# A ternary convolution's activations in SBUF: six pairs of quarter buffers for five, and one padded image for each channel half

## The chip, the cores and the metric

The kernel runs on one core of a Trainium2 chip. TensorE is called PE here, VectorE DVE, ScalarE ACT, GpSimd POOL and SyncE SP. PEld is PE's weight load. The metric is the device time of one execution in microseconds (us), of which lower is better. `L1357` is line 1357 of the kernel before.

## What is computed

Four layers follow each other on x of shape [4, 256, 64, 64] (images, channels, rows, columns), all in float32. Each is a residual layer behind a group normalisation:

```python
# --- layer 0: axial attention, 1: ternary conv, 2: binary grouped conv, 3: expanded conv
x = x + _L0_conv_ref(_gn(x), ...)
x = x + _L1_conv_ref(_gn(x), weight, alpha, bias)
x = x + _L2_conv_ref(_gn(x), ...)
x = x + _L3_conv_ref(_gn(x), ...)
```

The change lies in layer 1. Its weights take the values 1, 0 and -1 (times alpha):

```python
def _L1_conv_ref(x, weight, alpha, bias):
    delta = 0.7 * mean(abs(weight))
    ternary = where(w > delta, 1.0, where(w < -delta, -1.0, 0.0))
    w_t = ternary * alpha
    out = conv_general_dilated(x, w_t, (1, 1), padding=[(1, 1), (1, 1)])   # 3x3, NCHW
    return out + bias[None, :, None, None]

def _gn(v, G=32, eps=1e-5):     # over 8 channels and all rows and columns of one image
    return (g - mean(g)) / sqrt(var(g) + eps)
```

A group norm needs the sums of a whole image before the first row of that image can be normalised.

## The kernel before

The program runs the layers one after the other, each in a phase with buffer pools of its own. A pool takes its place in SBUF when it is opened, and a pool of a later phase may lie over the memory of an earlier one, whose last use it then waits for. The framework keeps the order of reads and writes on each buffer and arranges the instructions of each engine by its own scheduling, starting from the order in which the program emits them. So the lines below give the order of emission. The order on an engine can differ from it.

Layer 1 works on **quarters**: 16 rows of one image, 1024 pixels, in two channel halves t of 128 partitions. Four images of four quarters make 16 quarters, or 32 half quarters. The names are these:

- `load(b, t, q)` (L1264) makes x after layer 0 for one half quarter. It fetches the input into `dx` (L145, from `in_x`), fetches two attention results into `a` (two DMAs of L1276 for one, L145 for the other), scales one on ACT (L1279) and adds both to dx on DVE (L1281, L1284; the second also sums the pixels). `square` (L1262) sums the squares on ACT. All four DMAs of a load go through SP's queue.
- `row_of` (L1256) chooses the slot for dx: `2 * ((q - b) % 5) + t`, ten slots, which are five pairs. The slot of quarter (b+1, q) is therefore the one that quarter (b, q-1) had.
- `norm(b, ts)` (L1289) joins the sums of an image (L1298, and L1105 to L1110 in a helper), averages over groups with small matmuls on PE (`pst`, L115, L125 and L126) and forms scale and bias (L1303 to L1306).
- `transform(b, t, q)` (L1309) writes the normalised rows into a padded image `d_pad` on ACT (L1322: 16 rows, and one row from each neighbouring quarter), forms four combinations `dv` of 8x66 from them on DVE (L1324, L1328, L1329; a minimal-filtering scheme over rows), and splits these into `dh` (fp32r copy on ACT, L1334) and `dl` (what is left, on DVE, L1335).
- `chunk(b, q, co)` (L1340) makes one output half of one quarter: 48 matmuls 128x128 by 128x512 (L1357; four combinations, two input halves, dh and dl, three columns), the inverse combination (L1372 on ACT, L1373, L1374, L1376 on DVE), and the residual sum into dx (L1381). Then dx is written to `x2_d` for layer 2 (L1386), and for co = 1 to `z_d` as well (L1388). Both are DMAs of POOL's queue.

There are four padded images before: two with 18 rows for inner quarters (0 and 1, one for each half), and two with 19 rows for the first and last quarters of an image (2 and 3), in which the top or bottom row stays zero.

The loop (L1407 to L1418) emits, for each quarter (b, q), the loads of both halves of (b+1, q), the norm of the next image ahead of the last quarter, and then for each half the transform of the next quarter and the chunk of this one. The four loads of the first image stand ahead of the loop. A slot can be refilled only when L1386 and L1388 have read it.

Layer 2's phase (`e_` pools, from L1471) comes next. It reads x2_d and z_d back, and its first matmuls (L1451) take the operand `e_tr` (L1440).

Of the kernel before, what the change touches and what calls it, by code (L numbers as in the profile page):

```python
# [9 lines left out]
F32 = mybir.dt.float32  # L10
# [8 lines left out]
P = 128  # L19
B = 4  # L20
C = 256
HW = 4096
# [19 lines left out]
def network(ctx: ExitStack, tc, x, wqkv, relm, relt, relw, relv, counts, masks, vecs, rowv, ab, w1, l2w1, l2w2, l3w, mats, out):  # L42
# [4 lines left out]
    nc = tc.nc  # L47
# [94 lines left out]
    def load_shuffled(dst, src, t):  # L142

        rows = src.rearrange("(two i) f -> i two f", two=2)[64 * t : 64 * t + 64]
        nc.sync.dma_start(out=dst, in_=rows)  # L145
# [20 lines left out]
    with ExitStack() as ph:  # L166
# [112 lines left out]
        for b in range(B):  # L279
            xs, gm, rs = ready  # L280
            qs = [qp.tile([P, 8, 8, 64], F32, name=f"qs{t}_{b}", tag="qs") for t in range(2)]
            for k in range(NB):
# [49 lines left out]
                if k in (3, 7) and 2 * b + k // 4 - 1 in range(len(pieces)):  # L332
                    i = 2 * b + k // 4 - 1
# [76 lines left out]
    with ExitStack() as ph:  # L410
# [224 lines left out]
        for b in range(B):  # L635
            for gp in range(GP):
# [3 lines left out]
                q = qs[j]  # L640
                o = op.tile([P, 32, 64, 2], F32, name=f"o_{b}_{gp}", tag="o")
# [65 lines left out]
        s2, _ = bn_affine(sp, mean, var, row[:, 0:48], row[:, 48:96], 48)  # L707
# [36 lines left out]
    def from_scores(general, keep):  # L744
# [482 lines left out]
        with ExitStack() as ph:  # L1227
            ps_ = {
                k: pool(ph, f"d_{k}", {"a": 3, "o": 2}.get(k, 1))
                for k in "x2 x3 a x4 x5 x0 x6 p2 v0 h00 l00 u0 u1 x1 o s v1 h10 l10 h11 l11 p0 p1 p3 x7 x8 x9 h01 l01".split()  # L1230
            }
            ap_, op, sp = ps_["a"], ps_["o"], ps_["s"]
            wide = pool(ph, "d_ps3", 1, PSUM)
# [1 line left out]
            ring = [pool(ph, "d_ps", 2, PSUM)] * 2 + [wide]  # L1235
            taken = [0]

            pads = [
                ps_[f"p{i}"].tile([P, 18 + i // 2, 66], F32, name=f"d_pad{i}", tag="pad") for i in range(4)
            ]  # L1240
            u = [ps_[f"u{t}"].tile([P, 3, 4, C], F32R, name=f"d_u{t}", tag="u") for t in range(2)]
            for t in range(2):
                nc.vector.memset(pads[t][:, :, 0], 0.0)
                nc.vector.memset(pads[t][:, :, 65], 0.0)
                edge = pads[2 + t]
                nc.vector.memset(edge[:, 0:19:18, :], 0.0)
                nc.vector.memset(edge[:, 1:18, 0], 0.0)
                nc.vector.memset(edge[:, 1:18, 65], 0.0)

            def load_weights(t):  # L1250
                for dx in range(3):
# [2 lines left out]
            xs, vs, sums, mvs, norms, shift = {}, {}, {}, {}, {}, {}  # L1254

            def row_of(b, t, q):  # L1256
                xs[b, t, q] = ps_[f"x{2 * ((q - b) % 5) + t}"].tile([P, HW // 4], F32, name=f"dx_{b}_{t}_{q}", tag="x")
                return xs[b, t, q]

            def square(src, out):  # L1260
# [3 lines left out]
            def load(b, t, q):  # L1264

                if (b, t) not in sums:
                    sums[b, t] = sp.tile([P, 4, 2], F32, name=f"dst_{b}_{t}", tag=f"st{t}", bufs=2)
                xt = row_of(b, t, q)
                load_shuffled(xt, x[b][:, bass.ts(q, HW // 4)], t)
                if b == 0 and t == 1 and q == 0:  # L1270
                    for two in range(2):
                        prs[t, two] = value_norm(t, two, pst, "pst")
                a = ap_.tile([P, HW // 4], F32, name=f"a1_{b}_{t}_{q}", tag="a")
                for two in range(2):
                    src = at_d[1][b][t * P + 64 * two : t * P + 64 * two + 64].rearrange("i (k f) -> i k f", k=4)
                    nc.sync.dma_start(  # L1276
                        out=a[two:P:2].rearrange("p (k f) -> p k f", k=4), in_=src[:, :, bass.ts(q, 256)]
                    )
                nc.scalar.activation(a, a, AF.Copy, scale=prs[t, 1][:, 0:1])  # L1279
                xv = xt.rearrange("p (n k i) -> p n k i", k=4, i=16)  # L1280
                nc.vector.tensor_tensor(xv, a.rearrange("p (k n i) -> p n k i", k=4, i=16), xv, ALU.add)  # L1281
                a = ap_.tile([P, HW // 4], F32, name=f"a0_{b}_{t}_{q}", tag="a")
                load_shuffled(a, at_d[0][b][bass.ts(t, P), bass.ts(q, HW // 4)], 0)
                nc.vector.scalar_tensor_tensor(  # L1284
                    xt, a, prs[t, 0][:, 0:1], xt, ALU.mult, ALU.add, accum_out=sums[b, t][:, q, 0:1]
                )
                square(xt, sums[b, t][:, q, 1:2])

            def norm(b, ts):  # L1289

                if b not in mvs:
                    mvs[b] = small(sp, [P, 2, 2])
                for t in range(ts.start, ts.stop):
                    if b == 0:
                        shift[t] = small(keep, [P, 1])
                        nc.vector.tensor_tensor(shift[t], prs[t, 0][:, 1:2], prs[t, 1][:, 1:2], ALU.add)
                    whole_stats(sp, mvs[b][:, t, :], sums[b, t])
                    nc.vector.tensor_tensor(mvs[b][:, t, 0:1], mvs[b][:, t, 0:1], shift[t], ALU.add)  # L1298
                gm, rs = norm_stats(sp, pst, mvs[b], ts, M_GRPS, "d")
                for t in range(ts.start, ts.stop):  # L1300
                    i = t - ts.start
                    ra = small(sp, [P, 1])
                    nc.vector.tensor_tensor(ra, rs[:, i : i + 1], row[:, 96:97], ALU.mult)  # L1303
                    nb = small(sp, [P, 1])
                    nc.vector.tensor_tensor(nb, shift[t], gm[:, i : i + 1], ALU.subtract)
                    nc.vector.tensor_tensor(nb, nb, ra, ALU.mult)  # L1306
                    norms[b, t] = nb, ra

            def transform(b, t, q):  # L1309


                nb, ra = norms[b, t]
                edge = q in (0, 3)
                pad = pads[2 + t if edge else t]
                pad = pad[:, 1:19] if q == 3 else pad[:, 0:18]
                parts = [(xs[b, t, q].rearrange("p (h w) -> p h w", w=64), slice(1, 17))]
                if q > 0:
                    parts.append((xs[b, t, q - 1][:, 15 * 64 :].rearrange("p (h w) -> p h w", w=64), slice(0, 1)))
                if q < 3:
                    parts.append((xs[b, t, q + 1][:, 0:64].rearrange("p (h w) -> p h w", w=64), slice(17, 18)))  # L1320
                for src, rows in parts:
                    nc.scalar.activation(pad[:, rows, 1:65], src, AF.Identity, bias=nb, scale=ra)  # L1322
                v = ps_[f"v{t}"].tile([P, 4, 8, 66], F32, name=f"dv_{b}_{t}_{q}", tag="v")
                nc.vector.tensor_tensor(  # L1324
                    v[:, 0:4:3].rearrange("p k q w -> p q k w"), pad[:, 0:16].rearrange("p (q k) w -> p q k w", k=2),
                    pad[:, 2:18].rearrange("p (q k) w -> p q k w", k=2), ALU.subtract,
                )
                nc.vector.tensor_tensor(v[:, 1], pad[:, 1:17:2], pad[:, 2:18:2], ALU.add)  # L1328
                nc.vector.tensor_tensor(v[:, 2], pad[:, 2:18:2], pad[:, 1:17:2], ALU.subtract)  # L1329
                hi, lo = (  # L1330
                    ps_[f"{k}{(4 * b + q) % 2}{t}"].tile([P, 4, 8, 66], F32R, name=f"d{k}_{b}_{t}_{q}", tag="tr")
                    for k in "hl"
                )
                nc.scalar.copy(hi, v)  # L1334
                nc.vector.tensor_tensor(lo, v, hi, ALU.subtract)  # L1335
                vs[b, t, q] = hi, lo
# [67 lines left out]
            load_weights(1)  # L1404
            norm(0, slice(1, 2))
            transform(0, 1, 0)
            for b in range(B):  # L1407
                for q in range(4):
                    if b + 1 < B:
                        for t in range(2):  # L1410
                            load(b + 1, t, q)
                        if q == 3:
                            norm(b + 1, slice(0, 2))
                    nxt = (b, q + 1) if q < 3 else (b + 1, 0)
                    for co in range(2):
                        if nxt[0] < B:
                            transform(nxt[0], co, nxt[1])
                        chunk(b, q, co, b == q == co == 0)  # L1418
            lost = None
            if not general:  # L1420
                far = small(keep, [P, 1])
# [49 lines left out]
        with ExitStack() as ph:  # L1471
# [17 lines left out]
            pads = [[(padp if t == h == 1 else padq).tile([P, 34, 66], BF16, name=f"e_pad{t}{h}", tag=f"pad{t}{h}")  # L1489
                     for h in range(2)] for t in range(2)]  # L1490
# [6 lines left out]
            for i, p_ in enumerate((wp1, wp2)):  # L1497
                k = p_.tile([P, 2, 3, 4, 3, 64], BF16, name=f"e_k{i}", tag="k")
# [213 lines left out]
            _, sy2, cy2 = sums_affine(1, vec[:, V_G3 : V_G3 + 1], vec[:, V_B3 : V_B3 + 1])  # L1712


        with ExitStack() as ph:
# [37 lines left out]
            def finish_3(b, h, co, xh, sp, pst):  # L1753
                nc.gpsimd.dma_start(out=out[b, bass.ts(co, P), bass.ts(h, HW // 2)], in_=xh)

            set_up, load_weights, prepare, norm, transform, rest, sp, pst = conv_layer(
                "g", ph, u3_d, "a x0 x1 x2 x3 x4 x5 o u0 u1 t2 t3 t4 s t0 p0 p1 t1 t5", M_GRP, load_3,
                vec[:, V_L3B : V_L3B + 2], (1, 0), finish_3,
            )
# [131 lines left out]
```

## Time and profile before

| what | value |
|---|---|
| median of 3 runs | 2771.07 us |
| range of these runs | 2767.38 to 2775.86 us |
| the profiled execution | 2766.54 us |
| its span (first to last instruction) | 2764.8 us |
| mean granted TensorE clock | 0.937 |
| PE, share of the span busy | 87% |
| DVE, share of the span busy | 72% |
| ACT, share of the span busy | 44% |
| first and last matmul of L1357 | 1485.0 and 1908.9 us |

The profile is that of one execution, and its times count from its first instruction. The granted clock is the share of full speed that PE was allowed, and "busy" leaves out instructions that only issue DMAs or wait. Layer 1's convolution takes about 425 us of the span. The shares above are averages over all four layers and say little of this one stage.

### The profile page before, as it was taken

How to read it: one execution, taken by the hardware profiler on the slowest of the kernel's cores; microseconds unless marked ns; L12 is line 12 of the kernel's file. 1: busy time of each engine (PE TensorE's matmuls, PEld its weight loads, DVE VectorE, ACT ScalarE, POOL GpSimd, SP SyncE). 2: the span in 40 equal slices, each digit the busy share in tenths (PEclk: the TensorE clock that was granted, in tenths of full speed). 3: DMA queues.
4: the chain of work that ended last, by engine and by line, in shares of the span. 5: the costliest groups of instructions: out<-in, count | busy, mean ns of one | idle time of the engine just before them, and what ended most of it. 6: DMA issues, size and time to landing. Idle time of an engine off the chain costs nothing.

```text
span 2764.8 us, 78125 instructions
## 1 busy us (share of the span) xinstructions
PE 2398.3 (87%) x34632; PEld 1576.4 (57%) x34632; DVE 1980.3 (72%) x3362; ACT 1205.8 (44%) x1984; POOL 105.4 (4%) x201
## 2 busy tenths in 40 slices
PE   7999788888997888888773998998979859999998
PEld 4566555556665666666662776776545424444443
DVE  6665788988775466666558788885888877967742
ACT  4555355555555544555435466553448421110100
POOL 0000100000001000000000000000000000000000
PEclk9999899999999888899886999999989979999999
DMA  6766366666667777778776546524337742324110
GB/s 239 258 201 205 89 190 163 172 168 186 155 150 159 244 251 249 256 242 274 232 234 220 186 154 201 189 101 158 126 128 265 288 159 91 138 105 137 46 42 36
DMA packets 287996, 489.87 MB, mean 177 GB/s; under 512 B 32736, under 2 KB 149088, under 8 KB 274848
## 3 DMA queue, kind: packets, MB, share of 16 engines
q1 hardware_dynamic: 224992, 359.52, 42.9%
q10 hardware_dynamic: 48256, 58.73, 6.2%
q0 software_dynamic: 14400, 66.53, 6.1%
q8 instruction: 273, 4.47, 0.7%
q14 instruction: 75, 0.61, 0.1%
HBM read 281.46 MB, written 203.23 MB: 175 GB/s over the span
## 4 chain that ended last, share of the span: by engine, by line
issue 38%; PE 30%; DVE 14%; DMA 11%; ACT 5%; POOL 1%; SPq 1%; DVEq 0%; ACTq 0%; POOLq 0%
PE pd L505 5%; PE dc L1357 4%; PE po L293 3%; PE pv L308 3%; PE pq L526 3%; DMA at_d<-o_False 2%; PE e_False L867 2%; DMA x<-x_d 2%; PE pr_False L936 2%; DVE pt L877 2%; PE pe_False L970 2%; DMA dx<-in_x 2%; PE den_False L918 2%; PE pa_False L945 2%; PE pc L1451 2%
## 5 line engine op out<-in xcount | busy, mean ns | idle before, releaser
L1066 PE MATMUL gc<-gtr,g_u 128*128 128x512 f32 x1152 | 503.4, 599 | 11.3 <-DVE gtr L1044 6.7
L1066 PEld LDWEIGHTS gc<-gtr,g_u 128*128 128x128 f32 x1152 | 219.3, 191 | 287.3 <-issue 269.4
L512 DVE STREAM_TRANSPOSE t<-pd 128x1024 f32<-128x1024 f32 x256 | 304.5, 1229 | 86.0 <-PE pd L505 80.7
L505 PE MATMUL pd<-rm,qb 64*32 64x256 f32 x8192 | 305.5, 389 | 41.4 <-DVE t L512 32.3
L1451 PE MATMUL pc<-e_tr,e_k 128*64 128x512 bf16 x2304 | 265.3, 391 | 20.5 <-DVE e_tr L1440 13.3
L532 ACT ACTIVATE o<-pq 128x512 f32<-128x512 f32 x256 | 150.6, 594 | 267.0 <-PE pq L526 264.8
L1357 PE MATMUL dc<-dh,d_u 128*128 128x512 f32 x768 | 233.5, 414 | 33.9 <-ACT dh L1334 33.8
L505 PEld LDWEIGHTS pd<-rm,qb 64*32 64x32 f32 x8192 | 168.4, 108 | 134.7 <-DVE t L512 57.4
L907 ACT ACTIVATE pt<-pt,sm 128x512 f32<-128x512 f32 x256 | 162.7, 710 | 174.9 <-DVE pt L877 174.8
L1357 PE MATMUL dc<-dl,d_u 128*128 128x512 f32 x768 | 229.3, 408 | 0.4 <-DVE dl L1335 0.2
L1451 PEld LDWEIGHTS <-e_k 128*64 128x64 bf16 x2304 | 145.5, 112 | 137.2 <-issue 28.9
L526 PEld LDWEIGHTS pq<-t,t 64*64 64x64 f32 x8192 | 146.0, 138 | 86.1 <-issue 71.6
L526 PE MATMUL pq<-t,t 64*64 64x64 f32 x8192 | 168.5, 225 | 28.6 <-issue 23.5
L1357 PEld LDWEIGHTS dc<-dh,d_u 128*128 128x128 f32 x768 | 148.6, 195 | 74.9 <-ACT dh L1334 35.8
L877 DVE TENSOR_TENSOR pt<-e_False,si_False 128x1024 f32<-128x1024 f32 x128 | 151.6, 1216 | 34.6 <-PE e_False L867 34.3
L1357 PEld LDWEIGHTS dc<-dl,d_u 128*128 128x128 f32 x768 | 145.7, 191 | 42.2 <-DVE dl L1335 4.1
L1084 ACT COPY gc_c<-gc 128x512 f32<-128x512 f32 x32 | 18.6, 582 | 344.0 <-PE gc L1066 344.0
L867 PE MATMUL e_False<-qc_False,rw 32*128 32x256 f32 x1024 | 131.1, 481 | 27.4 <-DVE pt L877 15.8
L538 ACT ACTIVATE sq<-o 128x1024 bf16<-128x1024 f32 x128 | 135.5, 1059 | 4.0
L293 PE MATMUL po<-xg,wt 128*128 128x512 f32 x256 | 120.8, 611 | 6.1 <-DVE st L300 4.5
L970 PE MATMUL pe_False<-pt,ve 128*32 128x64 f32 x4096 | 91.4, 244 | 39.9 <-issue 31.8
L308 PE MATMUL pv<-wt,xg 128*128 128x256 f32 x512 | 120.0, 382 | 0.0
(403 smaller groups left out, 3604.5 us busy)
## 6 DMA issues: line engine op xcount, KB each, us to landing
si_False<-qk_d SPq DMA_DIRECT2D x64, 1024.0 KB
qk_d<-o SPq DMA_DIRECT2D x496, 128.0 KB
x<-x_d SPq DMA_DIRECT2D x32, 1056.0 KB
xa<-in_x SPq DMA_DIRECT2D x16, 1024.0 KB
vt_d<-vs ACTq DMA_DIRECT2D x32, 512.0 KB
q_d<-qs SPq DMA_DIRECT2D x64, 256.0 KB
qb<-q_d SPq DMA_DIRECT2D x128, 128.0 KB
qc_False<-q_d SPq DMA_DIRECT2D x64, 256.0 KB
```

The lines of the kernel that those rows point to most:

```text
L293: nc.tensor.matmul(psf, lhsT=wt[:, t, bass.ts(o, P)], rhs=xg[:, t, :], start=(t == 0), stop=(t == 1))
L308: nc.tensor.matmul(pv[:, j, :], lhsT=xg[:, t, pix], rhs=wt[:, t, C : 2 * C], start=(t == 0), stop=(t == 1),)
L505: nc.tensor.matmul(pds[t][32 * c : 32 * c + 32, m].rearrange("p j k -> p (j k)"), lhsT=q[rows, 2 * (gp % 2) + g, a, 32 * nb : 32 * nb + 32 ...
L512: nc.vector.transpose(ts[t][:, :, 32 * jh : 32 * jh + 32].rearrange("p a j b -> p j a b"), pds[t].rearrange("p m j k -> p j m k"),)
L526: nc.tensor.matmul(ps[nb][64 * g : 64 * g + 64, m, :], lhsT=ts[1][rows, n // 2, :, n % 2], rhs=ts[0][rows, n // 2, :, n % 2], start=True, ...
L532: nc.scalar.activation(o[:, :, n : n + 8, :], ps[nb].rearrange("p n (a b) -> p a n b", b=2), AF.Copy, accum_out=acc[:, nb, gp, col : col + 1],
L867: nc.tensor.matmul(es[x_ // 2][:, x_ % 2, :, :, par], lhsT=rw[rows, 63 - i : 127 - i].rearrange("p j r -> p (j r)"), rhs=q[rows, :, par, k ...
L877: nc.vector.tensor_tensor(dst, e, src, ALU.add)
L907: nc.scalar.activation(s, s, AF.Exp, scale=s2q[:, gp : gp + 1])
L1066: nc.tensor.matmul(ms[k], lhsT=u[t][:, dx, k, bass.ts(co, P)], rhs=vs[t][:, k, :, dx : dx + 64], start=(first and dx == 0), stop=(last and ...
L1357: nc.tensor.matmul(at[k], lhsT=u[t][:, dx, k, bass.ts(co, P)], rhs=v[:, k, :, dx : dx + 64], start=(first and p_ == 0 and dx == 0), stop=( ...
L1451: nc.tensor.matmul(m[64 * g : 64 * g + 64], lhsT=parts[:, g, i, k, dx, :], rhs=vs[g][:, k, 8 * (q % 2) : 8 * (q % 2) + 8, dx : dx + 64], s ...
```

## The change

- `row_of` has twelve slots in six pairs, taken in turn over all 16 quarters: `2 * ((4 * b + q) % 6) + t`.
- The two 19-row padded images are gone. One 18-row padded image for each half serves all quarters. Its columns are zeroed once, and its top or bottom row is zeroed in `transform` for the first and last quarter of an image.
- The quarter loaded in iteration n = 4b+q is n+5 where it was n+4. Its two halves are emitted one after each chunk, where both stood ahead of the quarter's work. The two halves of quarter (1, 0) are emitted ahead of the loop.
- The norm of the next image is emitted after the loads of its last quarter, at the end of iteration (b, 2), where it stood in iteration (b, 3) ahead of the chunks.
- The list of pools is changed to suit. The pools x0 to x11, p0 and p1 have other places in SBUF than x0 to x9 and p0 to p3 had.

```diff
--- before.py
+++ after.py
@@ -1227,7 +1227,7 @@
         with ExitStack() as ph:
             ps_ = {
                 k: pool(ph, f"d_{k}", {"a": 3, "o": 2}.get(k, 1))
-                for k in "x2 x3 a x4 x5 x0 x6 p2 v0 h00 l00 u0 u1 x1 o s v1 h10 l10 h11 l11 p0 p1 p3 x7 x8 x9 h01 l01".split()
+                for k in "x2 x3 a x4 x5 x0 x6 p0 v0 h00 l00 u0 u1 x1 o s v1 h10 l10 h11 l11 x7 x8 x9 p1 x10 x11 h01 l01".split()
             }
             ap_, op, sp = ps_["a"], ps_["o"], ps_["s"]
             wide = pool(ph, "d_ps3", 1, PSUM)
@@ -1235,17 +1235,11 @@
             ring = [pool(ph, "d_ps", 2, PSUM)] * 2 + [wide]
             taken = [0]
 
-            pads = [
-                ps_[f"p{i}"].tile([P, 18 + i // 2, 66], F32, name=f"d_pad{i}", tag="pad") for i in range(4)
-            ]
+            pads = [ps_[f"p{t}"].tile([P, 18, 66], F32, name=f"d_pad{t}", tag="pad") for t in range(2)]
             u = [ps_[f"u{t}"].tile([P, 3, 4, C], F32R, name=f"d_u{t}", tag="u") for t in range(2)]
             for t in range(2):
                 nc.vector.memset(pads[t][:, :, 0], 0.0)
                 nc.vector.memset(pads[t][:, :, 65], 0.0)
-                edge = pads[2 + t]
-                nc.vector.memset(edge[:, 0:19:18, :], 0.0)
-                nc.vector.memset(edge[:, 1:18, 0], 0.0)
-                nc.vector.memset(edge[:, 1:18, 65], 0.0)
 
             def load_weights(t):
                 for dx in range(3):
@@ -1254,7 +1248,7 @@
             xs, vs, sums, mvs, norms, shift = {}, {}, {}, {}, {}, {}
 
             def row_of(b, t, q):
-                xs[b, t, q] = ps_[f"x{2 * ((q - b) % 5) + t}"].tile([P, HW // 4], F32, name=f"dx_{b}_{t}_{q}", tag="x")
+                xs[b, t, q] = ps_[f"x{2 * ((4 * b + q) % 6) + t}"].tile([P, HW // 4], F32, name=f"dx_{b}_{t}_{q}", tag="x")
                 return xs[b, t, q]
 
             def square(src, out):
@@ -1310,9 +1304,9 @@
 
 
                 nb, ra = norms[b, t]
-                edge = q in (0, 3)
-                pad = pads[2 + t if edge else t]
-                pad = pad[:, 1:19] if q == 3 else pad[:, 0:18]
+                pad = pads[t]
+                if q in (0, 3):
+                    nc.vector.memset(pad[:, 0 if q == 0 else 17, :], 0.0)
                 parts = [(xs[b, t, q].rearrange("p (h w) -> p h w", w=64), slice(1, 17))]
                 if q > 0:
                     parts.append((xs[b, t, q - 1][:, 15 * 64 :].rearrange("p (h w) -> p h w", w=64), slice(0, 1)))
@@ -1404,18 +1398,20 @@
             load_weights(1)
             norm(0, slice(1, 2))
             transform(0, 1, 0)
+            for t in range(2):
+                load(1, t, 0)
             for b in range(B):
                 for q in range(4):
-                    if b + 1 < B:
-                        for t in range(2):
-                            load(b + 1, t, q)
-                        if q == 3:
-                            norm(b + 1, slice(0, 2))
                     nxt = (b, q + 1) if q < 3 else (b + 1, 0)
+                    far = divmod(4 * b + q + 5, 4)
                     for co in range(2):
                         if nxt[0] < B:
                             transform(nxt[0], co, nxt[1])
                         chunk(b, q, co, b == q == co == 0)
+                        if far[0] < B:
+                            load(far[0], co, far[1])
+                    if far[0] < B and far[1] == 3:
+                        norm(far[0], slice(0, 2))
             lost = None
             if not general:
                 far = small(keep, [P, 1])
```

## Prediction

> **What bounds the kernel now.** The change touches one stage of the program, the ternary convolution (L1228 to L1418), so I first found where that stage lies and what its bottleneck engine loses in it. On the page, the table of costliest groups gives the stage's two matmul groups. The number after the bar is busy time and mean duration, and the last part is idle time ahead of the group with what ended it:
>
> ```profile
> L1357 PE MATMUL dc<-dh,d_u 128*128 128x512 f32 x768 | 233.5, 414 | 33.9 <-ACT dh L1334 33.8
> L1357 PE MATMUL dc<-dl,d_u 128*128 128x512 f32 x768 | 229.3, 408 | 0.4 <-DVE dl L1335 0.2
> ```
>
> 1536 matmuls, and nearly all idle time ahead of them ends with one thing, the fp32r copy dh of L1334. Next I cut the stage (1485 to 1910 us) into stretches, PE's dc matmuls alone. Columns: window, its length, PE busy (count), granted clock, DMA share, GB/s.
>
> ```profile
> 1485.00:1515.00 30.00, 11.04 (x32) 0.61 0.63 200
> 1515.00:1597.50 82.50, 82.06 (x336) 0.98 0.55 182
> 1597.50:1616.00 18.50, 12.28 (x37) 0.82 0.23 69
> 1616.00:1702.50 86.50, 85.88 (x355) 1.00 0.63 206
> 1702.50:1720.00 17.50, 10.31 (x32) 0.80 0.40 129
> 1720.00:1803.00 83.00, 83.00 (x346) 1.00 0.57 189
> 1803.00:1822.00 19.00, 12.76 (x42) 0.82 0.12 50
> 1822.00:1910.00 88.00, 87.27 (x363) 1.00 0.39 140
> ```
>
> Undisturbed, 346 matmuls take 83.00 us: 0.24 us each, so 1536 need 369 of the 425 us, and inside an image PE is the bound. The rest is a start-up (first row) and three short windows, where one image of the batch gives way to the next. Each loses its length less its matmuls at 0.24: 18.5 − 37×0.24 = 9.6, 17.5 − 32×0.24 = 9.8, 19 − 42×0.24 = 8.9, **28.3 us together**. The timeline of PE at the first boundary shows both halves of such a loss, an idle gap and slow matmuls after it (in brackets: idle time and releaser):
>
> ```profile
> 1601.94 0.89 PE L1357 MATMUL dc<-dl,d_u 128*128 128x512 f32 x3
> 1608.53 2.50 PE L1357 MATMUL dc<-dh,d_u 128*128 128x512 f32 x5 [5.70 <-ACT dh L1334]
> ```
>
> Why dh is late is read backwards in the chain of waits (start, length, what):
>
> ```profile
> 1577.15 4.52 DMA dx<-in_x
> ...
> 1586.19 5.48 DMA dx<-in_x
> ...
> 1591.85 0.13 DVE dx L1281
> ...
> 1595.52 1.16 ACT dj L1262 x2
> ...
> 1597.58 0.38 PE pst L115 x2
> ...
> 1602.86 1.22 DVE dc_o L1376
> 1604.08 0.61 DVE dv L1328
> ```
>
> The last eighth of the next image lands at 1591.7, its additions and square end at 1596.7, the group statistics (PE at L115, DVE to L1306) at 1601.7, then pad rows, dv and dh to 1608.5. PE runs out of work at 1602.8. The load is that late because `load(b+1, t, q)` takes the slot that quarter (b, q−1) has only just left: in the same chain before 1572 the write-out of a quarter (3.77 and 6.32 us) stands directly ahead of an in_x load (4.08 and 1.91 us). SP's own waits agree:
>
> ```profile
> SPq L145 <- DMA x_d<-dx: 46.4, 8, 16.8
> SPq L145 <- DMA z_d<-dx: 31.0, 10, 14.4
> ```
>
> So the bound at a boundary is a serial chain of write-out, load, statistics and transform; it is not an engine's throughput.
>
> **What the Trainium skill says.** "TensorE: Matmul & The Clock Gate", Part 1, states that PE's clock falls to half after an idle window of about 3.4 us and returns after about as long a busy one. The trace agrees: after 5.70 us idle, 5 matmuls take 2.50 us where they need 1.2, and the clock of the three windows is 0.80 to 0.82. A gap cut to 1 or 2 us should lose its slow tail as well. "DMA: Bandwidth & Descriptors", Anatomy of one DMA, states that DMA engines don't wait on semaphores, the issuing sequencer does. The two SP lines show it: a load whose slot isn't free blocks the loads queued behind it on SP.
>
> **The change, part by part.** I read the new order of instructions on each engine from the two built programs, and put durations of this trace on it. T0 is the start of chunk (b,3,0); a chunk is 48×0.24 = 11.5 us, so dh of the next image is needed at T0+23.0.
>
> *Six pairs, loads five ahead, norm earlier.* The last load of image b+1 now reuses a quarter that left one chunk pair earlier, and its norm is emitted in iteration (b,2). On PE the matmul L115 of that norm stood after 30, 37 and 30 of the 48 matmuls of chunk (b,3,1) at the three boundaries; now it stands after 26, 47 and 41 of chunk (b,3,0): 52, 38 and 37 matmuls earlier, 12.5, 9.1 and 8.9 us. Simply shifted, the losses of 9.6, 9.8 and 8.9 would go almost to nothing. But DVE is busier where the norm now lies. Per half quarter it has L1281 1.14, L1284 1.21, L1324 1.17, L1328 and L1329 1.24, L1335 2.27, L1373 and L1374 1.20, L1376 1.15, L1381 1.15, bias 0.07: 10.6 us (each start to the next start), 92% of PE's 11.5. I replayed DVE, ACT and PE in the new order with these times. First boundary: statistics at 6.4, L1306 at 10.4, pads (1.24 and 0.43 us) to 12.5, dv to 15.0, dh at 17.1, the second half's dh at 25.1 where 24.4 is wanted: 0.9 us lost. Second: L1281 and L1284 of a load stand between L126 and L1306, which ends at 17.7; dh 24.4, dl 27.0, second dl 30.0: 4.9 lost. Third: L1306 14.8, pads behind an ACT square to 17.2, dh 21.7, dl 27.2: 2.3 lost. Sum 8.1 for 28.3: **−20 us**. Bounds: all of it (−28), or half kept (−14).
>
> *Loads in halves after the chunks.* Same DMAs, 4 for each half, same SP queue, not more of them; SP only meets them in another order. What is new is on DVE: dl of the second half now stands right behind L1281 of a load, so a late landing would hold dl and then PE. In the replay a landing has 3.8 to 5 us in hand before L1281's turn, with 9 to 10 us from L1381 to landing (write-out and load of the chain are 7.9 and 8.3 us, plus POOL's issue of about 1), and dl 2 to 2.5 us more before PE needs it. Cost taken +2 us over the stage for ill-fitting turns (bounds 0 and +8, the three boundary gaps apart). The L1281 waits of now (10.2 and 8.3 us) cost PE nothing, since DVE makes them up.
>
> *Pads.* Six memsets of the 19-row edge buffers at the start go; 16 one-row memsets (128x66) come on DVE. Nearest rows of the groups are today's memsets, 128x132 at 168 ns (L1246) and 128x17 at 73 ns (L1247): at most 16×0.17 = 2.7 us, two to a first or last quarter, inside the 0.9 us that DVE has spare in each half; 0 taken. With one pad for a half, the pad rows of the next quarter wait for L1324, L1328, L1329 of the one before, a whole quarter (23 us) earlier: 0. Without cover it would show ahead of L1322 only.
>
> *Start-up.* Two more loads (1,t,0) go ahead of the loop, behind the first image's eight. The new slots reach over memory that the attention phase leaves at 1459.4, while SP's neighbouring load waits until 1462.8 already: 0, bounds −0.5 and +1.
>
> *Tail.* The last matmul is at 1909, the next stage's first (L1451) at 1919.1. The slots' new places put the last quarter's buffer under the first operand e_tr of that stage, which must now await the write-out of L1386/L1388: L1381 ends at 1913.0, plus 3.8 to 6.3 us, against e_tr's 1907.6 now. +1 us taken, bounds −1 and +5.
>
> Sum: −20 + 2 + 1 = **−17 us**. The profiled execution is 2766.5 (span 2764.8 and 1.7 around it), 4.5 below the median of the runs, 2771.07; the sum on it gives 2749.5, on the median **2754**. About 0.3%, 8 us, is what a measurement of this kernel tells from no change.
>
> **Rivals.**
> *DVE becomes the bound.* For: 92%, and boundary work now falls into full halves. Against: L1376 waits 22.8 us for PE today, so DVE does have slack. If each boundary keeps half its loss (14 of 28.3) and the halves lose another 6: −8, 2763.
> *The earlier issue changes nothing*, because SP's queue blocks on a slot further ahead, and the last load lands as late as now: 2771. For: 132 us of SP waits on L1281. Against: the slot has been free a chunk longer.
> *Slower: the chain L1381, write-out, load lands late.* The statistics matmul sits in PE's own queue with about 70 matmuls of the old image behind it, and at the first boundary has no slack in the replay; dl sits behind L1281. If the 9 to 10 us became d longer, PE pays d at each of three boundaries and, beyond d = 6, d−6 at each of about 10 inner quarters. It breaks even near d = 6; at d = 8 it costs 24 + 20, so +27: 2798. For: a write-out of 6.32 us, and waits up to 16.8. Against: DMA share 0.55 to 0.63, and landings of 2 to 5.5 us.
>
> **How the numbers follow.** The working above 0.66 (2748 to 2760), DVE bound 0.16 (2763, half of it each side of the 0.3% line), no change 0.10, late chain 0.08. Faster 0.74, same 0.18, slower 0.08. The low end, 2746, is the boundaries wholly gone (−28) with the +3 kept; the high end, 2769, takes in the DVE rival and leaves out most of the last two.
>
> **What would show it.** Right: the three gaps under 5 us and the windows' clock near 1.00, the last dc matmul some 18 us nearer the first. Idle time before L1357 from dh at most 10 us of the 33.9, start-up's share left. Wrong: gaps released by pst L115 or dl L1335, new waits of DVE at L1281 above 20 us, e_tr released by z_d, or the same 5.7 us gaps.

## The result and the profile after

The changed kernel takes 2748.37 us, the median of 7 runs (2743.52 to 2757.16), where the kernel before takes 2767.38 us, the median of 7 runs (2757.49 to 2775.86). The ratio is 0.9927, with a 95% interval of 0.9905 to 0.9948: some 20 us, from 14 to 26. The forecast was a fall of 17 us.

In the changed kernel most lines of this stage have a line number that is smaller by 6 (L1357 is L1351, L1334 is L1328, L1281 is L1275, L1381 is L1375), and those of the next stage one that is smaller by 4 (L1451 is L1447, L1440 is L1436).

The groups of the stage by line and shape (busy time, mean ns of one, idle time ahead of the group and its releasers):

```profile
L1351 PE MATMUL dc<-dh,d_u 128*128 128x512 f32 x768 | 229.6, 407 | 15.6 <-ACT dh L1328 15.6
L1351 PE MATMUL dc<-dl,d_u 128*128 128x512 f32 x768 | 227.8, 404 | 4.1 <-DVE dl L1329 4.1
```

The idle time released by dh has fallen from 33.8 to 15.6 us. What is left of it are the two waits of the start-up, 7.14 and 8.48 us (7.25 and 8.61 before). The 4.1 us released by dl are new, and they lie at the second and third boundary. Here are PE's dc matmuls in stretches, the boundaries in the third, fifth and seventh row (window, length, PE busy and count, granted clock, DMA share, GB/s):

```profile
1489.80:1519.00 29.20, 9.16 (x31) 0.68 0.70 228
1519.00:1602.00 83.00, 83.00 (x334) 0.97 0.63 203
1602.00:1613.00 11.00, 11.00 (x47) 1.00 0.40 143
1613.00:1695.00 82.00, 82.00 (x339) 1.00 0.66 218
1695.00:1706.00 11.00, 8.09 (x33) 1.00 0.45 143
1706.00:1788.00 82.00, 81.98 (x338) 1.00 0.47 161
1788.00:1800.00 12.00, 11.20 (x46) 1.00 0.11 44
1800.00:1891.50 91.50, 90.58 (x375) 1.00 0.34 120
```

From the end of the start-up on, PE has hardly an interruption left, and the clock is 1.00 at all three boundaries, where it was 0.80 to 0.82. The first boundary is closed altogether. Reckoned as before, as length less 0.24 us for each matmul, the three windows lose 0, 3.1 and 1.0 us. The timeline of PE at the second shows the two waits that remain there (in brackets: idle time and releaser):

```profile
1699.91 0.96 PE L1351 MATMUL dc<-dh,d_u 128*128 128x512 f32 x3
1702.62 0.98 PE L1351 MATMUL dc<-dl,d_u 128*128 128x512 f32 x3 [1.75 <-DVE dl L1329]
1703.44 0.89 PE L1351 MATMUL dc<-dh,d_u 128*128 128x512 f32 x3
1705.48 0.98 PE L1351 MATMUL dc<-dl,d_u 128*128 128x512 f32 x3 [1.16 <-DVE dl L1329]
```

These waits are short, and the matmuls after them keep their pace: three take 0.89 to 0.98 us. With 1.16 us at the third boundary, 4.1 us of the 28.3 are left.

From the first dc matmul to the end of the last, the stage takes 401.1 us (1489.8 to 1890.9) where it took 424.3 (1485.0 to 1909.3). But part of that is given back at once. The chain of waits after the last dc matmul reads (start, length, what):

```profile
1891.00 1.21 DVE dc_o L1370
...
1894.28 11.36 DMA z_d<-dx
...
1905.73 0.72 DVE e_tr L1436
1906.45 0.14 issue
1906.59 1.46 PE pc L1447 x5
```

DVE can't write the next stage's first operand e_tr before the last quarter is written out, because both now lie at the same place in SBUF. That write-out takes 11.36 us, and the first pc matmul (the next stage's) starts 15.7 us after the last dc matmul, where it was 9.9. In the kernel before, pc stood right behind PE's last matmul on the statistics of the finished stage, L1424:

```profile
1918.97 0.19 PE L1424 MATMUL pbad<-mt,sm 128*1 128x1 f32 x2 [0.32 <-DVE sm L128]
1919.09 6.27 PE L1451 MATMUL pc<-e_tr,e_k 128*64 128x512 bf16 x30
```

In the changed kernel that matmul (now L1420) is done at 1901.4, and PE then waits 5.2 us for e_tr.

### The profile page after: what moved, and what is told of

It is laid out like the page before. It is cut to its first block, busy times and chain, and to the rows that moved or that the text cites. A ratio compares the mean times of both kernels' runs of the same rounds, so it can differ in the third digit from the quotient of the medians.

```text
span 2753.1 us, 78131 instructions
## 1 busy us (share of the span) xinstructions
PE 2399.8 (87%) x34632; PEld 1582.9 (57%) x34632; DVE 1978.8 (72%) x3372; ACT 1202.4 (44%) x1984; POOL 105.2 (4%) x201
## 5 line engine op out<-in xcount | busy, mean ns | idle before, releaser
L505 PE MATMUL pd<-rm,qb 64*32 64x256 f32 x8192 | 312.6, 396 | 44.2 <-DVE t L512 34.7
L1447 PE MATMUL pc<-e_tr,e_k 128*64 128x512 bf16 x2304 | 264.3, 390 | 24.3 <-DVE e_tr L1436 17.9
L1351 PE MATMUL dc<-dh,d_u 128*128 128x512 f32 x768 | 229.6, 407 | 15.6 <-ACT dh L1328 15.6
L1351 PE MATMUL dc<-dl,d_u 128*128 128x512 f32 x768 | 227.8, 404 | 4.1 <-DVE dl L1329 4.1
L1447 PEld LDWEIGHTS <-e_k 128*64 128x64 bf16 x2304 | 150.1, 112 | 135.4 <-issue 31.6
L1351 PEld LDWEIGHTS dc<-dh,d_u 128*128 128x128 f32 x768 | 146.0, 191 | 54.5 <-ACT dh L1328 16.1
L1351 PEld LDWEIGHTS dc<-dl,d_u 128*128 128x128 f32 x768 | 144.3, 189 | 44.8 <-DVE dl L1329 6.7
L867 PE MATMUL e_False<-qc_False,rw 32*128 32x256 f32 x1024 | 132.6, 481 | 30.8 <-DVE pt L877 15.7
L970 PE MATMUL pe_False<-pt,ve 128*32 128x64 f32 x4096 | 91.9, 245 | 31.5 <-issue 24.6
```

Source lines behind the costliest of these rows:

```text
L505: nc.tensor.matmul(pds[t][32 * c : 32 * c + 32, m].rearrange("p j k -> p (j k)"), lhsT=q[rows, 2 * (gp % 2) + g, a, 32 * nb : 32 * nb + 32 ...
L867: nc.tensor.matmul(es[x_ // 2][:, x_ % 2, :, :, par], lhsT=rw[rows, 63 - i : 127 - i].rearrange("p j r -> p (j r)"), rhs=q[rows, :, par, k ...
L1351: nc.tensor.matmul(at[k], lhsT=u[t][:, dx, k, bass.ts(co, P)], rhs=v[:, k, :, dx : dx + 64], start=(first and p_ == 0 and dx == 0), stop=( ...
L1447: nc.tensor.matmul(m[64 * g : 64 * g + 64], lhsT=parts[:, g, i, k, dx, :], rhs=vs[g][:, k, 8 * (q % 2) : 8 * (q % 2) + 8, dx : dx + 64], s ...
```

## The experiments

Below, the **stage** is the time from the first dc matmul to the end of the last, and the **tail** the time from there to the first pc matmul, both from each kernel's own profiled execution. One execution is one sample: two profiles of the same kernel differ by up to 4.4 us in the stage below. The kernel before has 424.3 and 9.9, the changed one 401.1 and 15.7. Ratios are to the kernel before, run on the same chip.

### Five pairs of slots, all else of the change kept

```diff
-  xs[b, t, q] = ps_[f"x{2 * ((4 * b + q) % 6) + t}"].tile(...)
+  xs[b, t, q] = ps_[f"x{2 * ((4 * b + q) % 5) + t}"].tile(...)
```

> The changed kernel with five pairs of slots again (4b+q mod 5 for mod 6), everything else of the change kept: one padded image for each half, halves loaded after each chunk, five quarters ahead. A load then takes the slot of the quarter whose chunk was emitted just before it. Theory (the gain is that the slot has been free a quarter longer): the statistics matmul L115 goes back into chunk (b,3,1), after 30 to 33 of its matmuls, the three gaps at the image boundaries come back at some 5 to 6 us each, the stage from the first dc matmul to the last takes 420 us or more for the 401 of the changed kernel, and the time is within 0.3% of the kernel before or up to 5 us above (tail). Rival (the gain is the earlier issue in halves or the pads): the boundaries stay closed and the ratio stays near 0.993.

The ratio is 0.9998 (0.9980 to 1.0017), the stage 423.4 us, the tail 10.1. The three gaps are back, as the timeline of PE shows:

```profile
1611.52 2.50 PE L1351 MATMUL dc<-dh,d_u 128*128 128x512 f32 x5 [5.70 <-ACT dh L1328]
...
1713.83 2.50 PE L1351 MATMUL dc<-dh,d_u 128*128 128x512 f32 x5 [5.74 <-ACT dh L1328]
...
1816.58 2.93 PE L1351 MATMUL dc<-dh,d_u 128*128 128x512 f32 x6 [5.70 <-ACT dh L1328]
```

In the list of waits (us in total, times, longest) DVE waits for the input again, 11 times:

```profile
DVE dx L1275 <- DMA dx<-in_x: 11.3, 11, 3.4
```

The kernel before had 8.3 us of these waits and the changed kernel has none. So loads five ahead, halves and shared pads together bring nothing without the sixth pair. There is a reason to be seen in the order of emission. The loads of the next image's last quarter stand at the end of iteration (b, 2) in the changed kernel and stood at the start of iteration (b, 3) before, which is the same point of the program but for the first half; and the norm follows them in both. A load wasn't moved forward. What changed is how long its slot has been free. With five pairs it takes the slot of the quarter whose chunk stands just ahead of it, with six that of the quarter before.

The traces show this directly. Counted from the start of chunk (b, 3, 0), the last load of the next image goes out 7.9 to 10.5 us later in the kernel before and 8.9 to 10.0 us later with five pairs, but 10.3 to 14.5 us earlier in the changed kernel. The statistics matmul L115 of that image is back after 33, 31 and 30 of the 48 matmuls of chunk (b, 3, 1), as expected. In the changed kernel it stands after 26, 47 and 41 of chunk (b, 3, 0), just as the prediction had read it from the program. The changed kernel's last loads, too, go out within 0.2 us of the landing of the write-out that frees their slot, so SP still waits for write-outs:

```profile
SPq L145 <- DMA x_d<-dx: 40.7, 9, 12.9
SPq L145 <- DMA z_d<-dx: 15.6, 9, 3.1
```

These are 56 us where the kernel before has 77, and with five pairs they are 57. The length of these waits is therefore not the measure of the gain: what the sixth pair changes is which write-out a load waits for.

The tail fits as well: with five pairs the last quarter lies elsewhere (x0 and x1), and the 10.1 us are those of the kernel before.

### Six pairs, but the loop of before

The loop of the kernel before (both halves of the quarter four ahead, at the start of an iteration) replaces the new one, and nothing is loaded ahead of the loop:

```diff
-  for t in range(2):
-      load(1, t, 0)
   for b in range(B):
       for q in range(4):
+          if b + 1 < B:
+              for t in range(2):
+                  load(b + 1, t, q)
+              if q == 3:
+                  norm(b + 1, slice(0, 2))
...
-              if far[0] < B:
-                  load(far[0], co, far[1])
-          if far[0] < B and far[1] == 3:
-              norm(far[0], slice(0, 2))
```

> Six pairs of slots and one padded image for each half, but the loop of the kernel before: both halves of the quarter four ahead loaded at the start of an iteration, norm after them. Theory (the sixth pair alone brings the gain): gaps at the boundaries of 2 us or less, dc stage of 400 to 405 us, ratio 0.991 to 0.996. Rival (the loads in halves, five ahead, bring it): gaps of 5 us return in part, stage above 410 us, ratio above 0.997.

The ratio is 0.9935 (0.9915 to 0.9954), the stage 402.5 us, the tail 16.1. The gaps in PE's timeline:

```profile
1698.49 1.68 PE L1351 MATMUL dc<-dh,d_u 128*128 128x512 f32 x6 [3.40 <-ACT dh L1328]
1701.08 0.99 PE L1351 MATMUL dc<-dl,d_u 128*128 128x512 f32 x3 [0.91 <-DVE dl L1329]
...
1796.61 0.99 PE L1351 MATMUL dc<-dl,d_u 128*128 128x512 f32 x3 [1.16 <-DVE dl L1329]
```

The first boundary is closed here too. The sixth pair with the old loop brings the gain within the measurement. L115 stands after 31, 45 and 44 matmuls of chunk (b, 3, 0), and the last load goes out 10.5 to 14.3 us ahead of that chunk, though SP's waits for write-outs are 85 us in all, longer than in the kernel before. One gap of 3.40 us is larger than the 2 us that I expected, so the halves may be worth some 1.4 us (5.5 us of gaps against 4.1). Neither the ratios nor one execution can tell that apart: a kernel below has 3.5 us of gaps at this boundary in one execution and 2.9 us in another.

### One padded image for each half, in the kernel before

```diff
-  pads = [ps_[f"p{i}"].tile([P, 18 + i // 2, 66], ...) for i in range(4)]
+  pads = [ps_[f"p{t}"].tile([P, 18, 66], ...) for t in range(2)]
...
-  edge = q in (0, 3)
-  pad = pads[2 + t if edge else t]
-  pad = pad[:, 1:19] if q == 3 else pad[:, 0:18]
+  pad = pads[t]
+  if q in (0, 3):
+      nc.vector.memset(pad[:, 0 if q == 0 else 17, :], 0.0)
```

> The kernel before with one padded image for each half and the row memsets in transform, its five pairs and its loop kept. Theory (pads cost and bring nothing): the three boundary gaps of 5.7 to 6.5 us stay, stage of 424 us within 3, ratio 0.998 to 1.002. Rival (sharing a pad makes the next quarter's rows wait for L1324 and L1329, or the memsets load DVE): waits of ACT at the pad rows for DVE dv above 5 us, time 3 to 8 us longer.

The ratio is 1.0004 (0.9988 to 1.0021). The stage, 427.9 us, is 3.6 longer than that of the kernel before, just outside the 3 us of the expectation and within what two profiles of one kernel differ by; the gaps at the boundaries are 5.74, 6.98 and 5.70 us. ACT does wait 6.4 us at the pad rows for L1318, as the rival said, but the total doesn't move. So the pads are neither gain nor loss that this measurement shows. What they give is room for the two new slots.

### Another place for the last quarter's buffer

The pools x1 and x7 have one size, so exchanging them in the list moves nothing else:

```diff
-  "x2 x3 a x4 x5 x0 x6 p0 v0 h00 l00 u0 u1 x1 o s v1 h10 l10 h11 l11 x7 x8 x9 p1 ..."
+  "x2 x3 a x4 x5 x0 x6 p0 v0 h00 l00 u0 u1 x7 o s v1 h10 l10 h11 l11 x1 x8 x9 p1 ..."
```

> The changed kernel with the places of pools x1 and x7 exchanged, so that the last quarter's second half no longer lies under the first operand e_tr of the next stage, which then lies over slots last used one to five quarters earlier. The instructions and their order stay the same. Theory (the changed kernel loses some 5 us at the tail to that overlap): DVE's wait at e_tr for z_d goes, the time from the last dc matmul to the first pc matmul falls from 15.7 us to about 10 to 11, and the kernel is about 5 us faster than the changed one, ratio to before 0.990 to 0.992. Rival (the tail is set by the load of x2_d or of the weights e_k anyway): the tail stays at 14 us or more with another releaser.

The ratio is 0.9923 (0.9894 to 0.9952), the stage 401.5 us and the tail 11.8, a little above the 10 to 11 expected. The wait of e_tr for z_d is gone. The write-out itself is nearly as long as in the changed kernel (10.9 us from issue to landing), but nobody waits for it, and the first pc matmul comes 0.12 us after the start of L1420 again. So the overlap is what made the tail long. In the time it isn't to be seen: the ratio lies just outside the 0.990 to 0.992 that I expected, and its interval takes in the changed kernel's 0.9927. In the next kernel x6, the last quarter's first half, moves too, behind v0:

```diff
-  "x2 x3 a x4 x5 x0 x6 p0 v0 h00 ..."
+  "x2 x3 a x4 x5 x0 p0 v0 x6 h00 ..."
```

> The changed kernel with pools x1 and x7 exchanged as in swap_x7 and, besides, x6 (the last quarter's first half) moved behind v0, into memory that the next stage needs last. Theory (what is left of the tail is the statistics of the last image on PE ahead of the first pc matmul, 11.8 us with x7 moved): no more than 1 us better than swap_x7, ratio to before 0.990 to 0.993. Rival (the load of x2_d into the place of x6 still holds the first operands): the tail falls from 11.8 us to 10 or less.

The ratio is 0.9900 (0.9871 to 0.9930). The tail of 10.9 us is within 1 us of the last kernel's, and pc again follows L1420 after 0.12 us, as the theory had it. But the stage was 405.2, longer than expected. The second boundary shows most of that:

```profile
1691.56 0.99 PE L1351 MATMUL dc<-dh,d_u 128*128 128x512 f32 x3 [1.07 <-ACT dh L1328]
1694.29 0.98 PE L1351 MATMUL dc<-dl,d_u 128*128 128x512 f32 x3 [1.75 <-DVE dl L1329]
...
1697.16 1.65 PE L1351 MATMUL dc<-dl,d_u 128*128 128x512 f32 x3 [0.70 <-DVE dl L1329]
```

The three gaps are 3.5 us together, and the matmuls after the third are slow: the granted clock is 0.53 from 1695 to 1700. So I ran this kernel once more, and the changed kernel beside it:

> The changed kernel once more, beside the two kernels with moved pools on the same chip. Theory: dc stage 401 us and tail 15.7 us within 1 us each, ratio 0.991 to 0.995.

> The kernel with x6 and x7 moved, once more. Theory (the tail's 4.8 us carry over to the end): tail within 1 us of 10.9, time 3 to 6 us under the changed kernel's median of the same call. Rival (they are lost again in the dc stage, which was 405 us in the first profile of this kernel for 401): stage 404 us or more again, time within 2 us of the changed kernel.

The changed kernel: stage 401.0, tail 16.2, median 2757.23 us (2744.81 to 2766.64), ratio 0.9918 (0.9897 to 0.9939). With x6 and x7 moved: stage 400.8, tail 10.0, median 2750.06 us (2747.14 to 2754.47), ratio 0.9892 (0.9875 to 0.9909). The end of the last dc matmul and the first pc matmul of the two in PE's timeline, first the changed kernel's, then that with moved pools:

```profile
1883.79 0.89 PE L1351 MATMUL dc<-dl,d_u 128*128 128x512 f32 x3
...
1900.89 59.33 PE L1447 MATMUL pc<-e_tr,e_k 128*64 128x512 bf16 x530 [4.90 <-DVE e_tr L1436]
```

```profile
1890.35 0.89 PE L1351 MATMUL dc<-dl,d_u 128*128 128x512 f32 x3
...
1901.28 58.93 PE L1447 MATMUL pc<-e_tr,e_k 128*64 128x512 bf16 x514
```

So the 405.2 was that one execution's, and the rival, a stage of 404 us or more again, is out. In the profiles the tail is shorter by 5 to 6 us. In the times the medians of these two lie 7 us apart (3 to 6 expected), but the intervals of the two ratios overlap. It is the best of the kernels here by its ratios and by its second profile, though these runs don't prove it faster than the changed kernel.

### A longer way from chunk to free slot

Each write-out is issued twice, so the slot comes free later. The result is the same data.

```diff
   nc.gpsimd.dma_start(out=x2_d[b][bass.ts(co, P), cols], in_=xq)
+  nc.gpsimd.dma_start(out=x2_d[b][bass.ts(co, P), cols], in_=xq)
   if co == 1:
       nc.gpsimd.dma_start(out=z_d[b]..., in_=xq)
+      nc.gpsimd.dma_start(out=z_d[b]..., in_=xq)
```

> The changed kernel with every write-out of a half quarter done twice (same data, x2_d and z_d), so that a slot comes free some 4 to 6 us later. The prediction's late-chain case (first boundary without slack, d of 4 to 6 us paid at each of three boundaries): gaps of 4 to 6 us return ahead of dc or pst, 12 to 18 us in all, ratio 0.997 to 0.9995. Rival (a slot that was left a quarter ago has over 6 us in hand): gaps as in the changed kernel within 2 us each, ratio 0.993 to 0.996, of which the tail takes a part, since its write-out is doubled too.

The ratio is 1.0068 (1.0042 to 1.0093): slower than the kernel before by some 19 us, and than both expectations. The stage is 430.8 us, the tail 20.7. The chain of waits ahead of the first boundary:

```profile
1559.00 1.24 DVE dx L1375 x2
...
1560.52 4.12 DMA x_d<-dx
1564.65 0.28 issue
1564.93 0.53 POOL x_d L1381
1565.46 2.00 issue
1567.47 5.32 DMA z_d<-dx
...
1572.92 4.18 DMA dx<-in_x
```

The second write goes to the same place as the first and waits for it on POOL (3.35 us in its timeline), so the two stand one after the other. From the end of L1375 (1560.2) to the landing (1577.1) it is 16.9 us where I had 9 to 10, so the delay d is about 7 us for this load. I had expected 4 to 6. What it does to PE is the prediction's late-chain case:

```profile
1591.27 0.59 PE L115 MATMUL pst<-sm,mt 128*128 128x2 f32 x2 [6.11 <-DVE sm L1292]
...
1662.93 1.65 PE L1351 MATMUL dc<-dl,d_u 128*128 128x512 f32 x3 [3.43 <-DVE dl L1329]
...
1717.97 1.65 PE L1351 MATMUL dc<-dh,d_u 128*128 128x512 f32 x3 [6.49 <-ACT dh L1328]
```

At the first boundary PE stands 6.11 us at the statistics matmul with the old image's products behind it, and within an image it waits for a dl behind a late L1275. The prediction's formula, 3d at the boundaries and d − 6 at ten inner quarters less the 17 of gain, gives 21 + 10 − 17 = +14 for d = 7, and with the 5 us by which the tail is longer than the changed kernel's, +19. The agreement of the sum is partly luck, since the gaps are spread less evenly than the formula has them. And the doubled writes also load the DMA engines, which this run doesn't separate. DVE's waits for the input (L1275) are 36 us here, where the changed kernel has none.

### More work for DVE

One (fill1) or two (fill2) additions of 128x512 on DVE follow L1368 in each chunk. Their result is not used.

```diff
   nc.vector.tensor_tensor(o[:, :, 1], c, mids[:, 1], ALU.subtract)
+  for _ in range(n):                                   # n = 1 or 2
+      idle = sp.tile([P, 8, 64], F32, ..., bufs=1)
+      nc.vector.tensor_tensor(idle, c, c, ALU.add)
```

> The changed kernel with one more DVE addition of 128x512 in each chunk, whose result is not used: 32 times some 0.62 us, 20 us of DVE work in the stage. If DVE still has the 0.9 us per half quarter that the sum of its rows leaves, most is covered: the stage of 401 us grows by 2 to 6 us, at the boundaries. Rival (DVE is already the bound, and PE's remaining waits for dl are its sign): the stage grows by 15 to 20 us.

> The changed kernel with two more DVE additions of 128x512 in each chunk, results not used: 40 us of DVE work in the stage, 11.8 us per half quarter with a load for PE's 11.5. If the sum of DVE's rows is right, DVE passes PE in the 22 half quarters that carry a load: about 7 us there and 5 to 10 more at the boundaries, stage 410 to 420 us. Rival (DVE is already the bound): 435 us or more. Rival (DVE has slack that the sum misses): under 408 us.

With one, the stage grows by 8.0 us to 409.1 (ratio 0.9932, 0.9906 to 0.9957); with two, by 13.9 us to 415.0 (ratio 0.9965, 0.9952 to 0.9978). fill2 is inside its expectation, fill1 above its 2 to 6 us and far below the rival's 15. DVE is close behind PE, then, and not the bound: of the added work, by the estimate of 0.62 us for one, 12 of 20 us are covered with one and 26 of 40 with two. The tails are shorter than the changed kernel's (12.3 and 11.8 us), so the times show less than the stages, and the ratio of fill1 can't be told from the changed kernel's. The second boundary shows how little it has in hand: with one addition the wait there is 3.52 us, and the six matmuls after it take 2.93 us, which six at full pace do in 1.6.

## Why the prediction was right, and where it wasn't

The time, the direction and the mechanism hold. Point by point, by its own terms:

| term of the sum | predicted, bounds | measured in the profiles |
|---|---|---|
| image boundaries | −20 (−28 to −14) | −24.2 (28.3 to 4.1) |
| halves, rest of the stage | +2 (0 to +8) | +1.0 (stage −23.2 in all) |
| start-up | 0 (−0.5 to +1) | −0.3 to the second start-up wait's end (29.4 to 29.15), within the row above |
| pads | 0 | not told from 0 (ratio 1.0004) |
| tail | +1 (−1 to +5) | **+5.8** (9.9 to 15.7) |
| sum | −17 | −17.3 from the first dc to the first pc matmul |

**The boundaries** came out 4 us better. The replay had 0.9, 4.9 and 2.3 us of loss, and the profile has 0, 2.9 and 1.2. The order of the three is as predicted, and what ends the waits, dl behind a busy DVE, too. At the second, the pads start at 1694.0, some 17.4 us after T0, where the replay has 17.7, but DVE begins the combination dv in the pads' first rows before the others are written, which brings dh and dl about 1 us earlier than in the replay. That a gap cut to 1 or 2 us loses its slow tail held for these gaps; in other kernels it didn't always (see the last section).

**The tail** is the step that failed. The prediction named the cause, e_tr under the last quarter's buffer, and took 3.8 to 6.3 us for the write-out, from earlier write-outs of the trace. It took 11.36 us, so the tail grew by 5.8 us, beyond the upper bound of 5. The view of DMA issues from 1880 to 1915 shows what ran beside it, the next stage's loads of x2_d and of its weights:

```profile
x<-x_d SPq DMA_DIRECT2D x6, 1056.0 KB
e_k<-bk_d SPq DMA_DIRECT2D x1, 1152.0 KB
z_d<-dx POOLq DMA_DIRECT2D x1, 512.0 KB, 11.4
```

The length of this write-out follows what the queue of these loads moved while it ran: 3.1 MB in the changed kernel, 2.9 MB where x7 was moved (10.9 us), 1.0 MB with one or two additions on DVE (7.5 and 7.0 us), 0.3 MB in the kernel before (4.2 us), and nothing where x6 was moved as well (3.8 us). In the changed kernel the DMA engines were 93% busy in these 11.4 us, so the write-out may have had to share them, but no run changed these loads alone. The two errors, −4 and +5, nearly cancel: that the sum is better than its parts is luck.

**The signs** that the prediction had named came out mixed. The gaps, the clock and the distance of the dc matmuls (23 us less for 18) are those of a right prediction. But the idle time from dh is 15.6 us where at most 10 were to be left: the start-up's share was taken too small, for it was 15.9 us before. And two of the signs of a wrong one appeared, gaps released by dl and e_tr released by z_d. The first is the small rest of the boundaries that the replay had, the second the tail.

**The reason given for the gain** was right in its core and loose at one point. The prediction counted "loads five ahead" and "norm earlier" beside the sixth pair as one edit. The five-pair and the old-loop kernels show that the sixth pair alone carries it, and that the place of emission hardly changed.

**The rivals.** DVE as the bound was held off, by some 0.4 to 0.8 us in each half quarter (12 and 26 us in 32); the prediction had 0.9. "The earlier issue changes nothing" is true of the issue, as it turned out, and false of the slot. The late chain didn't occur. The doubled write-out shows that it is the real danger to this schedule: with d of about 7 us it cost more than the gain. The break-even near d = 6 itself was not tried.

The total is less sharp than the stage. The profiled execution after is 2755.0 us, only 11.5 below that of before, because its attention phase ended 5.3 us later (the last L970 group starts at 1461.2 where it started at 1455.8). The medians of several runs depend less on such differences.

## What to carry to other kernels

Where a load waits for its buffer, ask first what the slot held last and how long that is done; one more pair of buffers was worth nearly all of the gain here (ratio 0.9935 alone, 0.9927 with the rest), and emitting loads five quarters ahead into the same five pairs was worth nothing. Don't judge a prefetch by how long its queue waits for free buffers, but by when the load lands against when it is needed. Paying for the room by merging buffers whose users lie a quarter apart cost nothing that was measured here. After any change in a list of pools, look at what the next stage's first operand now lies on: the exchange of two names of one size took 4 us off the tail in the profiles, and moving one more pool 5 to 6 us, though the run times don't prove either.

## What the hardware showed beyond what was expected

A write-out of 512 KB took 3.8 to 4.2 us from issue to landing when at most 0.3 MB of loads moved beside it, and 10.9 to 11.4 us beside 2.9 to 3.1 MB, so its duration in one stage says little of the next.

Whether the matmuls after a wait of PE are slow isn't told by the length of that wait alone. After 2.25 us (doubled write-outs), 2.75 us (fill2) and 3.40 us (six pairs with the old loop) they kept their pace, 0.24 us each. After 2.02 us (doubled write-outs) and 2.18 us (fill1) the first three did, but of the nine that followed most ran at half pace (up to 1.48 us for three). After 3.43 and 3.52 us (doubled write-outs, fill1), and after every longer wait of dc matmuls here, they were slow from the first on (three in 1.65, six in 2.93). And short waits close together can do it too: 1.07, 1.75 and 0.70 us, with three to six matmuls between them, were followed by three in 1.65 (first profile with x6 and x7 moved), where the changed kernel's 1.75 and 1.16 us were not. What decides it between 2 and 3.4 us stays open.
